# A search for row maxima moved behind both products in the attention sums of a transformer block

## The chip, the cores and the metric

The kernel runs on one core of one Trainium2 chip. The time is device microseconds of one launch, and lower is better. The five engines (TensorE or PE for matrix products, VectorE or DVE, ScalarE or ACT, GpSimd or POOL, SyncE or SP for transfers) each work through their own queue in order and wait for one another by semaphores.

## The reference, cut to what matters

The reference computes one adaptive-layernorm transformer block in float32: attention with eight heads of 32 columns over 4 batches of 2048 rows of 256, and after it a mixture of experts. The change lies in the attention:

```python
scores = jnp.einsum('bhqd,bhkd->bhqk', q, k) * scale
scores = jnp.where(causal[None, None], scores, -jnp.inf)
scores = scores + head_scales[None, :, None, None] * geo
attn = jax.nn.softmax(scores, axis=-1)
out = jnp.einsum('bhqk,bhkd->bqhd', attn, v).reshape(B, T, C)
```

Then come a second norm, two shared experts, the choice of 4 of 16 routed experts for each row, the rows' way to their experts and back, and the sum.

## The kernel before, in words

The rows are cut into 16 blocks of 512 queries, four blocks to a batch. Heads are taken four at a time (a "quad", `g` = 0 or 1). TensorE is a 128 by 128 array, and the four heads of a quad sit in four strips of it, so the four products of one kind run side by side.

Softmax is done in two passes. The **search** (`max_steps`, inner function `scores`) computes the scores of 128 queries against 512 keys with the queries in the partitions (tile `ps`), and VectorE reduces them to row maxima (tile `parts`); on the diagonal a mask is added first. One search step makes two `ps` tiles, of two heads each: eight matmul records on TensorE, then two reductions on VectorE, each behind a mask addition on the diagonal. A search covers the *next* block, so that its maxima are ready when that block's sums begin.

The **sums** (`sum_steps`) go through the keys in tiles of 128 (`kb`), with the keys in the partitions. `probabilities` (called `first` in the loop) makes the scores again into two tiles `st` of two heads each, subtracts the maxima by a further product (`mT`), and ScalarE takes the exponential of each tile into `p`. `weigh(kb, 0)` (`average`) multiplies `p` by the values into `av`, and `weigh(kb, 1)` (`total`) by ones into `dv`, which gives the softmax's denominator. Where there is room, `join` adds two `p` tiles on VectorE, and one product with ones then serves both.

All `ps` and `st` tiles, and small tiles of other steps that fall into the sums, take turns in one ring of three PSUM buffers, each of two banks (pool `mring`). So a new tile has to wait until the reader of the tile three turns earlier is done: a reduction for `ps`, an exponential for `st`.

TensorE's order is written out by hand. In the sums, each step is given a place, a number, and `run(part)` issues the steps sorted by it. A key tile owns one *slot* `n` (a whole number). Its scores stand at `n`, its product with values at `n + 1.3`, its product with ones at `n + 1.6` (or 2.55 where it is joined). So slot `m` runs: scores of tile `m`; at 0.1 a join; at 0.3 the product with values of tile `m - 1`; at 0.55 or 0.6 the product with ones; at 0.6 also the norms and the choice of experts (`put`); at 0.7 the turning of finished maxima (`turn`, tile `pr`); at 0.9 a step of the rows' transfers (`tick`).

```python
            for kb, (first, average, total) in enumerate(sums):
                n = g * half + kb
                part.append((n, first))
                part.append((n + 1.3, average))
                part.append((n + (2.55 if kb in joining else 1.6), total))
```

Between two blocks' sums stand the projections, the experts' products and most of the search (`fill_in`). Only the search steps left over there (`rest`) go into the sums; `at` spreads them over the slots. Of the 320 search steps 86 do so, in blocks 0, 1, 2, 3, 6, 7 and 10.

Of the kernel before, what the change touches and what calls it, by code (L numbers as in the profile page):

```python
# [94 lines left out]
def adaln_block_kernel(  # L95
# [1355 lines left out]
    for i in range(NBLK):  # L1451
# [4 lines left out]
        if i:  # L1456
# [21 lines left out]
            at = max(6, len(mid) - len(finals))  # L1478
# [40 lines left out]
        part = []  # L1519
        for n, (_, ss, turn) in enumerate(rest):  # L1520
            at = int(0.93 * (n + 0.5) / len(rest) * ks)
            part += [(at + 0.5, s) for s in ss]
            if turn is not None:
                part.append((min(at + 3.7, ks + 0.7), turn))
        part += [(2.7 + n, turn) for n, turn in enumerate(left)]
# [179 lines left out]
```

## Time and profile before

| | |
|---|---|
| median of 11 runs | 2458.79 us (2452.23 to 2477.46) |
| the profiled execution's own time | 2462.59 us |
| its span, first to last instruction | 2460.8 us |
| mean granted TensorE clock | 0.968 |
| TensorE busy | 2318.9 us, 94% |
| VectorE busy | 1435.1 us, 58% |
| ScalarE busy | 985.5 us, 40% |
| GpSimd busy | 732.9 us, 30% |

Every record of the main part bears line 54, since a helper class issues all instructions; so groups are told apart by tile names (`ps`, `st`, `av`, `dv`, `p`, `parts`). `PE` rows are matmuls, `PEld` rows the loading of their stationary operand. A float32 product has two matmul records for each head, so one step of four heads shows as x8. In the timeline the columns are start and duration in us, then engine, line, operation, and output<-inputs; square brackets give the idle time of the engine before the row, and what ended it.

### The profile page before, as it was taken

The numbers are of one execution on the slowest core, as the hardware profiler recorded it, in microseconds if no ns is written. First come the engines' busy times: TensorE is split into PE (matmuls) and PEld (weight loads), VectorE is DVE, ScalarE is ACT, GpSimd is POOL, SyncE is SP. The second block draws the span as 40 slices with busy tenths as digits, with TensorE's granted clock in tenths as the row PEclk, the third lists the DMA queues.
The fourth block names the chain that finished last, engine by engine and source line by source line (L and its number), as shares of the span: only waits on it lengthen the run. The fifth ranks groups of instructions, "written<-read, shape, count | busy, mean of one in ns | idle before, by whom it ended". The sixth has DMA issues, their size and how long they took to land.

```text
span 2460.8 us, 42187 instructions
## 1 busy us (share of the span) xinstructions
PE 2318.9 (94%) x16641; PEld 1134.7 (46%) x16641; DVE 1435.1 (58%) x2790; ACT 985.5 (40%) x1407; POOL 732.9 (30%) x740
## 2 busy tenths in 40 slices
PE   7999999999999999999999999997999998998998
PEld 4443433345554333354635434354544644436765
DVE  5666665536664775547665656847654675634325
ACT  2223343543334335534353344633334345552421
POOL 3201010331101344501023342601333125466325
PEclk9889999999999999999999999999999999999999
DMA  3200402243440212323524225222744844418953
GB/s 122 91 1 10 154 10 72 104 152 129 141 141 10 78 67 93 119 80 121 187 84 152 90 73 194 80 81 89 241 157 165 270 133 125 148 69 289 361 184 122
DMA packets 219830, 306.88 MB, mean 125 GB/s; under 512 B 18672, under 2 KB 158960, under 8 KB 219632
## 3 DMA queue, kind: packets, MB, share of 16 engines
q1 hardware_dynamic: 192720, 228.89, 28.1%
q0 software_dynamic: 25536, 73.43, 9.1%
q8 instruction: 131, 2.15, 0.4%
q10 hardware_dynamic: 1376, 1.86, 0.2%
q14 instruction: 67, 0.55, 0.1%
HBM read 193.49 MB, written 114.82 MB: 125 GB/s over the span
## 4 chain that ended last, share of the span: by engine, by line
PE 84%; DVE 5%; ACT 4%; issue 3%; DMA 2%; another core or an unknown queue 1%; POOL 1%; SPq 0%; ACTq 0%; DVEq 0%; POOLq 0%
PE st L54 18%; PE ps L54 13%; PE av L54 11%; PE dv L54 8%; PE pu L54 7%; PE py L54 6%; DVE parts L54 3%; PE ppq L54 3%; PE pv L54 2%; PE po L54 2%; PE px L54 2%; PE pd L54 2%; PE pd_s L54 2%; PE ppk L54 2%
## 5 line engine op out<-in xcount | busy, mean ns | idle before, releaser
L54 DVE TENSOR_REDUCE parts<-ps 128x2 f32<-128x1024 f32 (+3 forms) x640 | 662.7, 1063 | 349.0 <-PE ps L54 336.6
L54 ACT ACTIVATE p<-st 128x1024 f32<-128x1024 f32 (+3 forms) x640 | 539.1, 894 | 528.1 <-PE st L54 420.1
L54 PE MATMUL st<-qT,kv 32*128 32x512 f32 (+3 forms) x2560 | 413.9, 583 | 17.0 <-ACT p L54 12.1
L54 PE MATMUL ps<-kv,qT 32*128 32x512 f32 (+3 forms) x2560 | 381.5, 599 | 16.6 <-DVE parts L54 10.4
L54 POOL DMA_INDIRECT got<-yg,at x224 | 230.3, 1028 | 328.6 <-ACT p L54 108.2
L54 PE MATMUL av<-p,kv 128*32 128x512 f32 (+3 forms) x2560 | 305.0, 545 | 6.6 <-ACT p L54 3.2
L74 POOL DMA_INDIRECT xg<-rows,at x219 | 221.0, 1009 | 276.3 <-ACT p L54 105.5
L54 PEld LDWEIGHTS st<-qT,kv 32*128 32x128 f32 x2560 | 147.2, 186 | 276.3 <-issue 149.1
L54 PE MATMUL dv<-p,ones 128*32 128x512 f32 (+3 forms) x2224 | 255.6, 531 | 0.7 <-issue 0.7
L54 DVE TENSOR_TENSOR ps<-ps,cmask 128x256 f32<-128x256 f32 x256 | 109.3, 427 | 197.4 <-PE ps L54 162.0
L54 PEld LDWEIGHTS ps<-kv,qT 32*128 32x128 f32 x2560 | 124.3, 190 | 194.5 <-issue 87.2
L54 POOL TENSOR_TENSOR x<-x,tmps 128x512 f32<-128x512 f32 x28 | 35.4, 1263 | 493.5 <-DVE tmps L54 493.5
L54 PE MATMUL py<-wt,tact 128*128 128x256 f32 x608 | 164.3, 403 | 4.7 <-ACT xt L54 2.8
L54 PE MATMUL st<-mT,unit 3*128 3x512 bf16 (+3 forms) x1280 | 168.0, 346 | 0.0
L54 PEld LDWEIGHTS pu<-xt,wt 128*128 128x128 f32 x1216 | 149.1, 195 | 35.9 <-issue 17.8
L54 PE MATMUL pu<-xt,wt 128*128 128x128 f32 x1216 | 160.1, 284 | 2.3 <-DMA wt<-experts 1.6
L54 ACT COPY y<-py 128x512 f32<-128x512 f32 x152 | 89.0, 586 | 139.8 <-PE py L54 135.4
L54 PEld LDWEIGHTS py<-wt,tact 128*128 128x128 f32 x608 | 109.6, 195 | 55.9 <-ACT xt L54 15.5
L54 ACT COPY xt<-px 128x512 f32<-128x512 f32 x152 | 86.6, 586 | 114.3 <-PE px L54 109.3
L54 DVE TENSOR_TENSOR p<-p,p 128x1024 f32<-128x1024 f32 x84 | 105.2, 1293 | 43.2 <-PE av L54 35.7
L54 PEld LDWEIGHTS dv<-p,ones 128*32 128x32 f32 x2224 | 64.4, 110 | 133.0 <-issue 121.8
L54 POOL TENSOR_TENSOR xnb<-xnb,gm 128x256 f32<-128x256 f32 x128 | 104.8, 826 | 47.9 <-issue 19.7
(294 smaller groups left out, 2384.8 us busy)
## 6 DMA issues: line engine op xcount, KB each, us to landing
wt<-experts SPq DMA_DIRECT2D x304, 256.0 KB
xr<-xg SPq DMA_DIRECT2D x76, 512.0 KB
yg<-y SPq DMA_DIRECT2D x76, 512.0 KB
xg<-zeros SPq DMA_DIRECT2D x16, 1024.0 KB
xin<-in_x SPq DMA_DIRECT2D x16, 512.0 KB
x<-in_x SPq DMA_DIRECT2D x16, 512.0 KB
h2d<-xnb POOLq DMA_DIRECT2D x14, 512.0 KB
pre<-x POOLq DMA_DIRECT2D x14, 512.0 KB
```

The lines of the kernel that those rows point to most:

```text
L54: made = call(*args, **kwargs)
L74: made = call()
```

## The change

One number changes. A search step in the sums is placed at `at + 0.75` where it stood at `at + 0.5`:

```diff
         for n, (_, ss, turn) in enumerate(rest):
             at = int(0.93 * (n + 0.5) / len(rest) * ks)
-            part += [(at + 0.5, s) for s in ss]
+            part += [(at + 0.75, s) for s in ss]
             if turn is not None:
                 part.append((min(at + 3.7, ks + 0.7), turn))
```

In a slot it now comes behind the product with ones (0.55, 0.6), the norms and choices (0.6) and a turning (0.7), and ahead of the next tile's scores and of the transfers (0.9). In the built programs' instruction order this moves the search of 81 slots behind one product with ones (`av ps dv` becomes `av dv ps`); in four of these also behind a turning (`pr`), in three behind a small product of the choice (`pk`). The other 5 search steps of the sums stand in the first slot of a block, where no product precedes them, and keep their place. On VectorE the reductions move behind that slot's norms and choices. The orders of GpSimd's and SyncE's instructions are the same in both programs, and no instruction is added or removed.

## The prediction

> **What bounds the kernel now.** I read the page's busy shares and its chain of waits first, then the chain and the timeline inside one stretch of sums, row by row.
>
> ```profile
> PE 2318.9 (94%) x16641; PEld 1134.7 (46%) x16641; DVE 1435.1 (58%) x2790; ACT 985.5 (40%) x1407; POOL 732.9 (30%) x740
> ...
> PE 84%; DVE 5%; ACT 4%; issue 3%; DMA 2%; another core or an unknown queue 1%; POOL 1%; SPq 0%; ACTq 0%; DVEq 0%; POOLq 0%
> ```
>
> TensorE is busy 94% of the span and holds 84% of the chain that ends last. What is put into its queue, or left waiting there, is paid in full unless something else was late as well. The chain in two slots of block 6's sums that hold a search:
>
> ```profile
> 884.51 1.63 PE st L54 x10
> 886.15 0.99 PE av L54 x8
> 887.14 1.11 PE ps L54 x8
> 888.26 1.00 PE dv L54 x8
> 889.25 1.62 PE st L54 x10
> ```
>
> A slot is 4.73 us, all of it TensorE. But the scores take 1.62 us here, and 1.29 in slots without a search (chain at 1015.95), so some waiting hides in a row that counts as busy. The timeline of single rows tells which:
>
> ```profile
> 887.07 1.18 PE L54 MATMUL ps<-kv,qT 32*128 32x512 f32 x8
> 888.19 1.07 PE L54 MATMUL dv<-p,ones 128*32 128x512 f32 x8
> 888.25 1.23 DVE L54 TENSOR_REDUCE parts<-ps 128x2 f32<-128x1024 f32 x1 [1.39 <-PE ps L54]
> 889.18 1.48 PE L54 MATMUL st<-qT,kv 32*128 32x512 f32 x8
> 889.53 0.30 PEld L54 LDWEIGHTS st<-qT,kv 32*128 32x128 f32 x4
> ```
>
> The first reduction ends at 889.48 (888.25 + 1.23). Heads 0 and 1 of the next scores begin at 889.18, the loads for heads 2 and 3 at 889.53, 0.05 us after that reduction. So those two heads wait for the first `ps` tile, which held the third buffer of the ring, and they start 0.35 us after the others. From the search's start to that release are 2.46 us (889.53 - 887.07). On the diagonal it is later still:
>
> ```profile
> 1012.50 0.96 DVE L54 TENSOR_REDUCE parts<-ps 128x2 f32<-128x768 f32 x1
> ...
> 1012.90 0.30 PEld L54 LDWEIGHTS st<-qT,kv 32*128 32x128 f32 x4 [0.84 <-issue]
> ...
> 1013.58 0.22 PEld L54 LDWEIGHTS st<-qT,kv 32*128 32x128 f32 x2 [0.38 <-issue]
> ```
>
> Here the mask's addition (0.43 us, from 1012.04) stands ahead of the reduction, which ends at 1013.46; heads 2 and 3 load at 1013.58, 0.68 us behind heads 0 and 1. I went through the 81 slots in which the search will change places. In 70 the second half of the scores starts behind the first like this, by 0.17 to 2.20 us; in 4 both start together, just as that reduction ends or later; the 7 with a `pr` or `pk` between are taken singly below. The product with ones stands exactly between the search and the scores that wait for it: it is the cover.
>
> **What the change does, part by part.** It adds and removes no instruction.
>
> The cover goes. From the search's start to the release remain 2.46 us, but of TensorE's work only the search itself (1.1 us) and heads 0 and 1 are left to fill them. The next scores' second half starts about 1.4 us behind its first, for 0.35 before. The product's time comes ahead of the search and pushes search, reduction and release back by its length.
>
> How long that is, two pairs of rows tell:
>
> ```profile
> 1005.61 1.07 PE L54 MATMUL av<-p,kv 128*32 128x512 f32 x8
> ...
> 1006.49 1.90 PE L54 MATMUL dv<-p,ones 128*32 128x512 f32 x16
> ...
> 1010.01 1.06 PE L54 MATMUL av<-p,kv 128*32 128x512 f32 x8
> ...
> 1011.00 0.97 PE L54 MATMUL ps<-kv,qT 32*128 32x384 f32 x8
> ```
>
> From `av` to `dv` are 0.88 us, from `av` to `ps` 0.99: a change between the two shapes of tile costs 0.11. In the new order `av` and `dv` follow each other (0.88), then `dv` to `ps` takes 1.00, so the search starts 0.88 later, not 1.00. The second change saved, between `ps` and `st`, lies inside the wait and is worth nothing. A full slot becomes 1.27 us (scores' second half to `av`) + 0.88 + 1.00 + 2.46 = 5.61 us for 4.73. The narrower products, at 1044.9 to 1048.3, take 0.67 (384 queries), 0.45 (256) and 0.22 (128).
>
> The Trainium skill, "TensorEngine Tiling (Array Packing)", section "Key Properties", says that changing the tiling mode drains TensorE. It speaks for the change: the new order changes twice less in each slot. If both savings counted, 81 x 0.11 = 9 us would come off the sum below; the rows say that one of them falls into the wait.
>
> The sum over the 81 slots, by the width of the product: 65 x 0.88 = 57.2, 8 x 0.67 = 5.4, 5 x 0.45 = 2.3, 3 x 0.22 = 0.7, together 65.6 us. Corrections:
>
> - Four slots with a turning. Before, `pr` took a buffer behind the search, and the next scores' second half waited for the *second* reduction (3.59 us from the search's start at 327.08, 2.45 at 1384.20). After, `pr` (0.33) comes ahead: 0.88 + 0.33 + 2.46 against 3.59 is +0.1, and for the narrow one (release 1.65 after its start) +0.4. Two of each give 1.0 for the 3.5 counted: -2.5.
> - Three slots with `pk` (0.44): it was cover too, and both halves came just as the reduction ended: about +1.3, +1.3 and +0.7, for 2.6 counted: +0.7.
> - One slot (862.5) in which the search's second tile already waits for an exponential until 3.41 us into the slot: the product slips into that wait, -0.3 for +0.7: -1.0.
>
> That leaves 62.8 us. VectorE's moved steps I cost at nothing: the norms and choices at 0.6 now stand ahead of the reductions, but VectorE waited 1.39 us for the search in the row above, and that grows by 0.88; the code allots such slots 1.4 us. ScalarE is not late either: its second exponential ends 3.19 us after the scores' second half began (892.72 against 889.53), and the search that needs its first now starts 3.15 us after it, the scores that need its second 4.2 us after it. Behind the waiting scores are queued the maxima's product, `av`, `dv` and the next search, and ScalarE's exponentials, so the loss is passed on and not made up. Of waits elsewhere that a later TensorE could shorten there are few (the largest are `px` for a DMA, 4.3 us at 1478, and `pta` for ScalarE, 4.4 at 1301); I take 1.5 off.
>
> The profiled run takes 2462.6 us, so 2462.6 + 61.3 = 2523.9; it is 3.8 above the median of the runs. Against the median: **2520 us**, 2.5% slower.
>
> **The rivals.**
>
> *VectorE is late as well, or the clock falls.* If the steps now ahead of the reductions are not done when the search is, the release comes later by the rest. It decides once such work takes more than the 2.3 us (1.39 + 0.88) that VectorE would have idle. Slot 836.5 shows the size: there split, choices and a sum of rows made the reduction start 1.8 us late. Were every fifth of the 81 slots like it, 16 x 1.8 = 29 us more: 2549. Against it: no other of the 81 was late by over 0.4 us before. Likewise more stalls could lower the granted clock. It was 1.00 in the stretch from 291 to 393, where nearly every slot has the short stall, and 0.97 from 1373 to 1464. Three per cent of the 527 us of these stages is 16 us: 2536. The Trainium skill, "TensorE: Matmul & The Clock Gate", section on PSUM-queue depth-cycling, warns of micro-idles between matmul groups at bank turns; it prices none, and the 1.00 above speaks against it.
>
> *Faster.* If the second half of the scores found its buffer free in time (the reduction's end and the loads' start agreeing by chance), both changes of tile shape saved would count: 81 x 0.22 = 18 us, 2441. It decides where the stall is nil before and after. The constant 0.05 or 0.15 us from reduction to load, in slots whose reductions start anywhere from 1.2 to 3.0 us after the search, excludes chance for most.
>
> *Part is made up.* If half of the loss fell on time in which TensorE would have waited anyhow, it would be 31 us: 2490. the matmuls' named waits are short: none is over 13 us in total.
>
> *Nothing measurable* (within 0.3%, 7.4 us, about what can be told from no change here): gains and losses would have to cancel, 2459.
>
> **How the numbers follow.** My forecast: 0.77. Its lower end is 2504, 45 us (65.6, corrections doubled to -5.6, and -15 for all the waits of `px`, `pta` and `ptb` behind these blocks); its upper end 2536, 77 us (no corrections, and six slots as late as that at 836.5, 6 x 1.8). VectorE or clock, 2536 to 2560: 0.09. Part made up, 2466 to 2504: 0.08. Nothing: 0.02. Faster: 0.04. The range from 2500 to 2545 takes in the first, half of the second and the upper end of the third. Faster by over 0.3% is 0.04, within 0.02, slower 0.94.
>
> **What would show it.** In the profile after: slots such as the one at 884 should be 5.6 us long in the chain, with order `av`, `dv`, `ps`, `st`, and a score piece of about 2.7 us. The load of heads 2 and 3 should still start 0.05 us behind the first reduction's end, 2.46 us after the search began, and 1.3 to 1.4 us after heads 0 and 1. `av` to `dv` should be 0.88, the reduction's idle time ahead of it longer than 1.39. Blocks 1 and 2 and 6 and 10 should carry nearly all of the loss (13, 20, 20 and 13 slots), blocks 4, 5, 8, 9 and from 11 on none. I am wrong if the scores' second half starts with its first, if VectorE has no idle time ahead of the reductions, or if a stretch without search in its sums gets longer.

## The result, and the profile after

The changed kernel takes **2538.64 us** (median of 16 runs, 2530.56 to 2541.72). The kernel before took 2463.1 in 62 runs beside it, and the ratio is 1.0295, 95% interval 1.0274 to 1.0316: about 3% slower. The profiled execution took 2537.04 us (span 2535.3) against 2462.59 (2460.8), so there are 74.5 us of span to find.

The page of the kernel after: busy time and share by engine, the chain by engine, and the group of the scores (busy time, mean of one, then the engine's idle time ahead of it and what ended it).

```profile
PE 2338.6 (92%) x16641; PEld 1145.4 (45%) x16641; DVE 1436.4 (57%) x2790; ACT 985.1 (39%) x1407; POOL 731.5 (29%) x740
...
PE 80%; DVE 8%; ACT 4%; issue 3%; DMA 1%; another core or an unknown queue 1%; POOL 1%; SPq 0%; ACTq 0%; DVEq 0%; POOLq 0%
...
L54 PE MATMUL st<-qT,kv 32*128 32x512 f32 (+3 forms) x2560 | 451.1, 583 | 70.7 <-DVE parts L54 54.7
```

VectorE's share of the chain went from 5% to 8%, with the same busy time. The idle time ahead of the scores was 17.0 us before, most of it ended by ScalarE's `p`; now it is 70.7, and 54.7 of it ends with a reduction. The scores wait for the reduction of the search. One slot of block 6 in the chain of waits (start, length, what):

```profile
937.68 0.81 PE st L54 x4
938.49 1.00 PE av L54 x8
939.49 0.86 PE dv L54 x8
940.35 1.08 PE ps L54 x8
941.43 0.02 issue
941.45 1.24 DVE parts L54
942.69 0.04 issue
942.73 0.41 PE st L54 x2
```

The order is `av dv ps st`, as the diff says, and a reduction now stands in the chain in 73 of the 81 moved slots; before it did in 11. The next slot's `av` is at 944.08, so the slot takes 5.59 us (944.08 - 938.49) where it took 4.73. The timeline of the same slot shows who waits:

```profile
937.15 0.70 PE L54 MATMUL st<-qT,kv 32*128 32x512 f32 x2 [0.47 <-DVE parts L54]
...
938.42 1.07 PE L54 MATMUL av<-p,kv 128*32 128x512 f32 x8
...
939.30 1.04 PE L54 MATMUL dv<-p,ones 128*32 128x512 f32 x8
...
940.28 1.14 PE L54 MATMUL ps<-kv,qT 32*128 32x512 f32 x8
...
941.24 1.02 PE L54 MATMUL st<-qT,kv 32*128 32x512 f32 x4
...
941.45 1.23 DVE L54 TENSOR_REDUCE parts<-ps 128x2 f32<-128x1024 f32 x1 [1.91 <-PE ps L54]
```

From `av` to `dv` are 0.88 us, from `dv` to `ps` 0.98. Heads 0 and 1 start 0.96 after the search (941.24), heads 2 and 3 only at 942.73, which is 2.45 after the search and 1.5 after the first half. TensorE as a whole stands still for some 0.5 us of that (0.47 in the row of 937.15); for the rest half of its rows work alone. VectorE idled 1.91 us ahead of the reduction, 1.39 before: it is not late.

So far this is the predicted picture. The granted clock is not. The windows view (stretch, its length, busy time of PE, PEld, DVE, ACT, POOL, granted clock, DMA share, GB/s), for block 2's sums and for two neighbouring pieces of them:

```profile
302.00:430.00 128.00, 114.09 (x846) 38.07 (x849) 66.52 (x116) 43.92 (x52) 7.68 (x10) 0.95 0.18 61
...
400.00:403.20 3.20, 2.38 (x16) 0.61 (x16) 2.69 (x4) 0.36 (x1) 0.00 (x0) 0.99 0.00 0
403.20:406.60 3.40, 3.40 (x20) 0.81 (x16) 0.00 (x0) 1.58 (x2) 0.00 (x0) 0.51 0.00 0
```

The clock over this stretch was 1.00 before (291 to 393) and is 0.95 now. In one 3.4 us window it is about half, and that window follows 3.2 us in which TensorE was busy for only 2.38 us, 74%. The timeline of TensorE there:

```profile
401.60 0.70 PE L54 MATMUL st<-qT,kv 32*128 32x512 f32 x2 [0.82 <-DVE parts L54]
...
402.87 1.72 PE L54 MATMUL av<-p,kv 128*32 128x512 f32 x8
404.35 1.96 PE L54 MATMUL dv<-p,ones 128*32 128x512 f32 x8
406.23 1.28 PE L54 MATMUL ps<-kv,qT 32*128 32x512 f32 x8
```

A search on the diagonal, with the mask's addition ahead of the reduction, made TensorE stand for 0.82 us. After it `av` to `dv` takes 1.48 us and `dv` to `ps` 1.88, for 0.88 and 0.98.

**Where the 74.5 us are.** I measured each slot from `av` to `av` in both profiles and added up the records of the granted clock.

| part of the difference | us |
|---|---|
| the 81 moved slots, at full clock (75 slots that were at full clock in both, 55.8, scaled to 81) | +60.3 |
| 33.6 us more at half clock within the sums that hold searches (14.4 before, 48.0 after), half of it lost | +16.8 |
| other slots of the sums at full clock | -0.4 |
| the stretches between the sums | -2.8 |
| sum | +73.9 |

The second row is an upper estimate, as it takes TensorE to be the bound in all of that time. The block times (from a block's first scores to its last) bear it out: the sums of blocks 0, 1, 2, 3, 6, 7 and 10 grew by 3.0, 10.9, 21.8, 7.7, 13.9, 5.9 and 13.2 us, together 76.4, which is 16.1 more than the slots at full clock.

Not all of the second row comes from the new stalls. The clock's records change only at multiples of 3.41 us, and ten slow spells begin inside these sums. In the 3.41 us ahead of each, TensorE was busy for 43 to 76%. Seven of the ten follow a wait in a moved slot, of 0.82 to 2.28 us; they last 3.41 us each, 24 us together, 21 of them within the second row; about 10 are lost. The other three follow a wait of 1.58 to 1.81 us for ScalarE at the start of a block's sums. The kernel before has the same three waits, and in blocks 3 and 7 its clock fell behind them too. In block 2 it did not: there the wait was divided between two of the clock's windows, each 73 to 74% busy, and now it lies in one, 47% busy. An eleventh spell, at the start of block 10's sums, lasts 13.65 us for 6.83 before. A poorly filled window is not always followed by a slow one: of 34 windows in these sums with TensorE busy for 76% or less, ten were.

### The profile page after: what moved, and what is told of

It is laid out like the page before. It is cut to its first block, busy times and chain, and to the rows that moved or that the text cites. A ratio compares the mean times of both kernels' runs of the same rounds, so it can differ in the third digit from the quotient of the medians.

```text
span 2535.3 us, 42184 instructions
## 1 busy us (share of the span) xinstructions
PE 2338.6 (92%) x16641; PEld 1145.4 (45%) x16641; DVE 1436.4 (57%) x2790; ACT 985.1 (39%) x1407; POOL 731.5 (29%) x740
## 4 chain that ended last, share of the span: by engine, by line
PE 80%; DVE 8%; ACT 4%; issue 3%; DMA 1%; another core or an unknown queue 1%; POOL 1%; SPq 0%; ACTq 0%; DVEq 0%; POOLq 0%
PE st L54 17%; PE ps L54 12%; PE av L54 11%; PE dv L54 8%; PE pu L54 7%; PE py L54 6%; DVE parts L54 5%; PE ppq L54 2%; PE px L54 2%; PE pv L54 2%; PE po L54 2%; PE pd L54 2%; PE pd_s L54 2%; PE ppk L54 2%
## 5 line engine op out<-in xcount | busy, mean ns | idle before, releaser
L54 PE MATMUL st<-qT,kv 32*128 32x512 f32 (+3 forms) x2560 | 451.1, 583 | 70.7 <-DVE parts L54 54.7
L54 PE MATMUL ps<-kv,qT 32*128 32x512 f32 (+3 forms) x2560 | 374.0, 598 | 16.2 <-DVE parts L54 10.4
L54 PE MATMUL av<-p,kv 128*32 128x512 f32 (+3 forms) x2560 | 313.3, 558 | 7.4 <-issue 3.8
L54 PEld LDWEIGHTS st<-qT,kv 32*128 32x128 f32 x2560 | 156.1, 187 | 342.5 <-issue 164.0
L54 PEld LDWEIGHTS ps<-kv,qT 32*128 32x128 f32 x2560 | 118.5, 190 | 192.6 <-issue 103.3
L54 PE MATMUL st<-mT,unit 3*128 3x512 bf16 (+3 forms) x1280 | 174.5, 351 | 0.0
L54 PEld LDWEIGHTS dv<-p,ones 128*32 128x32 f32 x2224 | 74.0, 113 | 127.4 <-issue 117.2
L54 PEld LDWEIGHTS av<-p,kv 128*32 128x32 f32 x2560 | 54.2, 109 | 145.4 <-issue 119.0
```

Source lines behind the costliest of these rows:

```text
L54: made = call(*args, **kwargs)
```

## The experiments

The theories are named as in the expectations. **A**: the scores' second half waits for the first reduction, and the product with ones no longer covers that. **B**: VectorE is late, because norms and choices now stand ahead of the reductions. **C**: the new stalls make the clock fall, and that is a cost of its own. The kernel before takes from 2426 to 2469 us on the different chips of these runs, so each ratio is to the runs of the kernel before on the same chip, and times are compared only within a chip.

### VectorE's order alone, and the product's place alone

The first kernel is the one before with the norms and choices ahead of the search. On TensorE only the small products `pk` of three slots move, ahead of the search; the product with ones stays behind it.

```diff
-                part.append((at + 0.6, step))
+                part.append((at + 0.45, step))
```

> The VectorE half of the change alone: the norms and choices move from 0.6 to 0.45, ahead of the search, which stays at 0.5; on TensorE the product with ones stays behind the search. Theory A (the product with ones was cover for the wait on the first reduction): ratio to before 1.000 within 0.003; only the three small products of the choice cost about 0.4 us each. Theory B (the norms and choices ahead of the reductions make VectorE late): most of the loss, 1.02 to 1.03.

Measured: 2430.48 against 2425.59, 1.0015 (1.0002 to 1.0029). The slots at full clock sum to +0.7 us. VectorE's new order costs next to nothing; B falls.

The second is the changed kernel with the norms and choices behind the search again (`at + 0.6` to `at + 0.8`), so that against the kernel before the product with ones changes sides, and in four slots the turning, but VectorE's order does not.

> The TensorE half alone: the search at 0.75 as in the change, the norms and choices moved behind it to 0.8, so VectorE reduces ahead of them as before. Theory A: the whole loss, ratio 1.027 to 1.031 (about 2535 us). Theory B: 1.000 to 1.005.

Measured: 2500.77, 1.0314 (1.0296 to 1.0331), with +56.8 us in the moved slots at full clock, for 60.3 in the changed kernel. Nearly the whole loss comes with the place of the product. Of the other 3.5 us 1.7 stand in the three slots with `pk`, whose place differs between the two kernels.

### Shorter reductions: take the wait away

In both orders the reductions in the sums read only the first quarter of the columns, so the maxima are not those of all keys. Nothing else is touched.

```diff
-                    parts[:, t, 2 * a : 2 * a + 2, ch], both[:, :, :w], AX.X, ALU.max
+                    parts[:, t, 2 * a : 2 * a + 2, ch], both[:, :, : w // 4 if state["summing"] else w], AX.X, ALU.max
```

> The kernel before, but in the sums the reductions read only a quarter of the search's columns (the maximum is then that of a subset; the softmax's shift changes, the work on TensorE does not). The reduction falls from 1.23 to about 0.42 us, so the release comes 1.65 us after the search's start, ahead of the scores at 2.1. Theory A: the waits of 0.35 to 1.0 us of the 81 slots go, 35 to 45 us, ratio 0.981 to 0.987. Theory B: VectorE has time to spare as it is, 1.000.

> The changed kernel with the same short reductions. Theory A: the release comes 0.88 + 1.65 us after where the search used to start, 0.4 us behind the scores in plain slots and 0.9 in diagonal ones: 35 to 50 us slower than quarter_early in place of 74, ratio to before 0.997 to 1.008. Theory B (moved norms and choices): the difference stays near 74 us.

Measured against 2469.33: the early order 2434.98, 0.9853 (0.9809 to 0.9897); the late one 2460.52, 0.9965 (0.9938 to 0.9992). The two orders stand 25.5 us apart where the full reductions left some 66 to 74. A reduction of 128x256 takes 0.43 us in these runs against 1.23, which is what makes the release earlier, and with it most of the loss goes: A is shown. From the late kernel's timeline:

```profile
950.51 0.43 DVE L54 TENSOR_REDUCE parts<-ps 128x2 f32<-128x256 f32 x1
```

More of the loss went than I had expected (35 to 50 us were to be left). The slots alone differ by 36 us (+3.1 against -33.1), as expected. In the two profiled executions the late kernel spent 147 us of its span at half clock and the early one 165 (from their mean clocks, 0.970 and 0.966), which gives back about 9. Over all runs of the two the mean clocks are nearer, 0.967 and 0.965, which gives back 3 to 4; the rest of the difference between 36 and 25.5 is open.

The early kernel also shows that the order *before* was not free of this wait: 33.1 us of it were left in these slots.

### Filling the stall with useless products

If C holds, TensorE work that the answer doesn't need may make the changed kernel *faster*, as long as it lies in the stall. Here the second `ps` tile's products of each search in the sums are made twice, with the same operands into the same place:

```diff
+            if state["summing"]:
+                for u in range(2):
+                    r = G * (2 + u)
+                    nc.tensor.matmul(
+                        halves[1][:, u, :w],
+                        lhsT=qTs[i][r : r + G, g, t * P : (t + 1) * P],
+                        rhs=kT[r : r + G, (i - qb + ch) % SLOTS, g, :w],
...
+                    )
```

> The kernel before with the same doubled products. Theory A: there the wait is only 0.35 us in a plain slot and 0.6 to 1.0 in diagonal ones, so 0.6 us of the 0.96 show in some 36 plain slots and 0.2 to 0.4 in the others: 25 to 40 us, ratio 1.010 to 1.016. Without a wait 78 us, 1.032.

> The changed kernel, but in the sums the products of the search's second tile are made twice: 0.96 us more of TensorE work in each of 86 slots, between the search and the waiting scores, 0 to 83 us if all of it showed. Theory A: it falls into the 1.39-us wait, so the time is that of the changed kernel, 2538 within 6 us, ratio to before 1.028 to 1.033. If there is no wait there, 2538 + 78 = 2616, ratio 1.06. If waiting lowers the clock (theory C: the 12 us by which the forecast fell short are extra half-clock windows of 3.41 us), it could come out up to 12 us lower, with fewer such windows.

Measured: on the order before, 2450.99 against 2425.59, 1.0101 (1.0084 to 1.0118): the extra products cost 25 us. On the changed order, 2487.23, 1.0243 (1.0225 to 1.0262), which is 13.5 us *less* than the 2500.77 of the kernel with only the product moved, on the same chip. Its slots at full clock lost as much as that one's (59.0 against 56.8), so the gain isn't there; its total at half clock was 133.6 us against 162.3, and half of that difference is 14.4. The other runs agree: the mean clock over the four of each kernel is 0.975 against 0.967.

Inside the searched sums, though, the half clock had hardly moved in that pair's profiles (39.3 against 42.1); most of the difference lay elsewhere, and why isn't known. So I repeated it beside the unaltered changed kernel:

> The changed kernel, on the same chip as the next: ratio 1.028 within 0.004. Theory C: its profile again has half-clock windows that begin in the slot behind a diagonal search of 384 keys, where TensorE's records fill only 0.76 of the 3.4 us before (slots 1_1_4, 2_1_6, 3_1_5 or their like), and some 40 to 55 us of such windows in the sums that hold searches.

> The changed kernel with the search's second tile multiplied twice, as in twice_late. Theory A: the added 78 us of TensorE work cost nothing in the 81 slots, so no slower than late_third. Theory C: the windows behind the 384-key slots are gone, and the time is 5 to 14 us below late_third. If the earlier difference between two chips was the reason, the two agree within 3 us.

Measured against 2428.09: the changed kernel 2509.27, 1.0323 (1.0290 to 1.0357); with the useless products 2483.56, 1.0236 (1.0202 to 1.0269). They make it faster by 25.7 us, more than expected. The slots at full clock lose the same (57.9 and 59.0). At half clock are 180.0 us against 121.8 in all, and within the searched sums 53.3 against 6.5; half of those 46.8 us is 23.4. The windows view of the two kernels for the same stretch of the program, which holds block 2's sums, first the changed kernel, then the one with useless products:

```profile
300.00:449.00 149.00, 134.24 (x1001) 50.03 (x1003) 78.17 (x138) 49.72 (x63) 12.00 (x14) 0.95 0.17 57
```

```profile
300.00:443.00 143.00, 129.72 (x1081) 50.35 (x1079) 76.05 (x136) 49.71 (x63) 11.78 (x14) 0.99 0.16 54
```

The first has 80 matmul records fewer and takes 6 us longer, at a clock of 0.95 for 0.99. The timeline of the kernel with useless products shows where they went:

```profile
918.93 0.59 PE L54 MATMUL st<-qT,kv 32*128 32x512 f32 x2
918.95 0.59 PE L54 MATMUL ps<-kv,qT 32*128 32x512 f32 x2
...
920.43 0.70 PE L54 MATMUL st<-qT,kv 32*128 32x512 f32 x2 [0.46 <-DVE parts L54]
```

The extra `ps` products run beside the first half of the scores, in the other rows of the array, and the second half still waits for the reduction as before (0.46 us of idle time for 0.47). Stall and slot are the same in these slots, 5.59 us in the chain (on the diagonal the longest stalls fall from 1.5 or 1.7 us to 1.1); what differs is the clock. C is shown: a part of the loss is the clock's, and work in the half-empty array takes it away. Between those two kernels nothing else was changed, and it does not hang on the two profiles: the clock is 0.964 to 0.966 in the four runs without the useless products and 0.969 to 0.976 in the four with them. Not all of the 46.8 us in the searched sums is their work, though: some 20 follow waits for ScalarE at the start of a block's sums, which are as long in the other profile (1.58 to 1.81 us) and are followed by no slow window there.

### The changed kernel again

> The changed kernel again, for the comparison on one chip and for its half-clock windows: ratio 1.0295 within 0.003. Theory C (stalls bring more half-clock windows): its profile again shows some 25 us more of throttled time than the kernel before (185 to 159), several of them inside the sums of blocks 1, 2, 3, 6, 7 and 10. If that was chance, the windows in the sums go.

Measured: 2535.04 against 2469.33, 1.0253 (1.0210 to 1.0296), less than expected. The slots at full clock lost 60.1 us, as in the first profile (60.3); at half clock were 195.1 us in all and 54.8 in the searched sums. The ten slow spells of the first profile are all there again, three of them behind a search of 384 keys on the diagonal, and two more, in block 0.

But the expected 25 us of half clock more than in the kernel before did not come on this chip. The granted clock of every run is on record. Put together for all runs of a chip (half clock in us is twice the span times what the mean clock lacks of 1), it tells what the clock adds to the slots:

| kernel | mean clock, before and after | more at half clock, us | half of it | loss measured less the slots' loss |
|---|---|---|---|---|
| the changed kernel in this section (2469 us before) | 0.962, 0.963 | 3 | 2 | 65.7 - 60.1 = 5.6 |
| only the product moved (2426 us before) | 0.973, 0.967 | 37 | 18 | 75.2 - 56.8 = 18.4 |
| the changed kernel beside useless products (2428 us before) | 0.972, 0.965 | 39 | 20 | 81.2 - 57.9 = 23.3 |

The slots' loss is always taken against the one profile of the kernel before; the kernel with VectorE's order alone, at +0.7 us on another chip, shows how little the chip changes these slots. So the slots' part is the same wherever it was measured, 57 to 60 us, and the clock's part goes from nearly nothing to some 20 us. Where it adds nothing, the kernel before already spends as much time at half clock (some 186 us) as the changed one (189).

### The search ahead of both products

If the product with ones is cover, both products would cover more:

```diff
-            part += [(at + 0.5, s) for s in ss]
+            part += [(at + 0.2, s) for s in ss]
```

> The search placed the other way, at 0.2, ahead of both products. Theory A: two products (2.0 us) now cover the reduction and the next scores wait for nothing; but the search's second tile has to wait for the first exponential of the same slot, with no product to fill that: about 0.45 us a slot, 25 to 45 us slower than before, ratio 1.010 to 1.018. If cover behind the search were all that counts: faster than before by its waits, 0.983.

Measured: 2490.61 against 2469.33, 1.0088 (1.0059 to 1.0117), slower than the order before, a little less than expected. The timeline of this kernel in block 6:

```profile
905.45 1.02 PE L54 MATMUL ps<-kv,qT 32*128 32x512 f32 x4
...
906.78 1.13 PE L54 MATMUL ps<-kv,qT 32*128 32x512 f32 x4 [0.31 <-ACT p L54]
...
909.69 0.31 PEld L54 LDWEIGHTS st<-qT,kv 32*128 32x128 f32 x8 [0.84 <-issue]
```

The scores that follow now load all four heads together, so the wait of before is gone. A new one has come: the search's second tile needs the buffer that the scores left only a moment ago, and waits for ScalarE's exponential, 1.33 us behind the first tile. The slot is 5.43 us (904.26 to 909.69). Of the three places the one between the products is the fastest. In these slots the search needs a product ahead of it, for the buffer it takes, and one behind it, for the buffer it gives back.

### The mask by products: a version that beats both

The stalls left in the order before are longest on the diagonal, where VectorE adds the mask ahead of each reduction. Here TensorE adds it, by four products with a constant, for the diagonal searches of 384 and 512 keys in the sums (21 steps):

```diff
+            by_product = state["summing"] and ch == qb and w > 2 * P
...
+            if by_product:
+                for both in halves:
+                    for u in range(2):
+                        nc.tensor.matmul(
+                            both[:, u, w - P : w], lhsT=kmask, rhs=ident_b, start=False, stop=True
+                        )
...
-                if ch == qb:
+                if ch == qb and not by_product:
```

> The kernel before, but in the sums the diagonal's mask (for searches of 384 and 512 keys) is added by four small products on TensorE in place of two additions of 0.43 us on VectorE. Theory A: what counts is the time from the search's start to the end of its first reduction. It falls from 2.94 to about 2.67 us in 12 slots of 512 keys and from 2.59 to about 2.2 in 7 of 384, while TensorE's added 0.33 us lies inside the wait: 5 to 6 us faster than before, ratio 0.9975 within 0.0015. If TensorE's own work counts instead: 21 x 0.33 = 7 us slower, 1.003.

Measured: 2417.95 against 2428.09, 0.9951 (0.9934 to 0.9968). The same slot in the chain of the kernel before, then in this one:

```profile
370.26 0.99 PE av L54 x8
371.26 0.90 PE ps L54 x8
372.16 1.00 PE dv L54 x8
373.15 1.97 PE st L54 x10
```

```profile
371.23 0.99 PE av L54 x8
372.23 1.23 PE ps L54 x12
373.46 0.99 PE dv L54 x8
374.45 1.29 PE st L54 x12
```

The search costs 0.33 us more on TensorE and the scores 0.68 less: 4.51 us for 4.86. Some 19 such slots at -0.36 are 7 of the 10 us, which is already more than the 5 to 6 expected. For the rest the clock is enough: it was 0.974 over all runs against 0.972, some 11 us less at half clock. No run separates the two.

## Why the prediction was right, and where it fell short

The measured 2538.64 lies inside the range of 2500 to 2545, but 18.6 above the forecast of 2520 and 2.6 above the upper end that the sum itself gave (2536). The range holds it because it took in half of the rival with VectorE and the clock. Of the 18.6 us 4.3 are the kernel before, which took 2463.1 beside it where the forecast had set out from 2458.8.

**The cover.** Right, and shown. The release comes 2.45 us after the search's start (2.46 predicted), the second half of the scores 1.5 after the first (1.3 to 1.4), and with shorter reductions most of the loss goes.

**The price of a slot.** 5.58 to 5.59 us for the 5.61 predicted. The medians by the product's width are 0.86, 0.64, 0.43 and 0.22 us; 0.88, 0.67, 0.45 and 0.22 were put down. That only one of the two changes of tile shape would count held too: the first half starts 0.96 behind the search and not 1.06 or so, but that only makes its wait longer. Of the two readings weighed for the Trainium skill's drain of TensorE, the one by the rows was right.

**The corrections.** Turnings: +0.39, +0.06, +0.06, +0.39 (0.4, 0.1, 0.1, 0.4). Slots with `pk`: +1.33, +1.33, +0.71 (1.3, 1.3, 0.7). The slot that waited for an exponential: -0.20 (-0.3). The 81 slots together: 60.3 for 62.8.

**VectorE at nothing.** Right: its idle time ahead of the reductions grew from 1.39 to 1.91 and 2.41 us, and its new order alone measured 1.0015.

**Waits elsewhere.** The stretches between the sums became 2.8 us shorter (1.2 to 4.6, by where the sums are taken to end); 1.5 was taken off. The time at half clock outside the searched sums fell too, by 7 us (144.2 to 137.2), so how much of it the waits gave back isn't known.

**Where it falls.** Blocks 1, 2, 6 and 10 carry 59.8 of the 76.4 us, 78%: "nearly all" was too much said for 66 of 81 slots. The sums without searches stayed within some 2 us.

**The step that failed: the clock.** The sum had no term for it. In the profiled execution it was worth up to 16.8 us, some 10 of them behind the new waits; the miss there is 13.2 (74.5 measured, 61.3 predicted). It is no fixed cost: where the changed kernel was run again, it came to some 2 us. The rival that held it, "Three per cent of the 527 us of these stages is 16 us", had the size right but the wrong odds, and it was set up as another case, not as an addition to the forecast. The argument against it was "the 1.00 above speaks against it". That clock was granted to slots whose second half came 0.35 us late, with TensorE never quite idle. It said nothing of slots in which half of the array is empty for 1.5 us and all of it for 0.5 to 0.8, in some for up to 2.3. The profile before had a sign against it: behind a wait of 1.59 us for ScalarE, at 417.0 and again at 942.3, the clock fell to half for 3.4 us. The stretches that made up its 527 us begin, there, only at 423 and at 948, when most of these two spells is over. The Trainium skill, "TensorE: Matmul & The Clock Gate", section "A second HAM failure mode: psum-queue depth-cycling", was cited there and set aside. The runs side with the page: the kernel without and with TensorE work in those gaps has 53.3 and 6.5 us at half clock in the searched sums. How full TensorE must be is not settled: 76% preceded a slow window, and 54% was in one place followed by none.

**The rivals.** VectorE late: fell. Faster: fell, as the stall grew in nearly every slot. Part made up: fell, as some 200 other slots of the sums moved by 0.4 us together.

## What to carry to other kernels

A product that seems to stand in the way between a search and the next scores may be the time in which the search's buffer is read: before moving it, measure from the producer's start to the release of the buffer, and see which work is left to fill that. Where a change makes TensorE wait more often, price the clock in the sum as well, and take the evidence for it from stretches with stalls of the new length, not of the old. Where both neighbours of a step can be late, try both sides, and then shorten what the buffer's reader does.

## What the runs showed of the hardware

- The clock can fall while TensorE is mostly busy. In the changed kernel's profile a 3.4 us window at half speed followed one in which TensorE's records filled 74%, with no whole-engine pause over 0.82 us; others followed pauses of up to 2.28 us. The loss was some 1.65 us in that slot (7.2 to 7.3 us for 5.6).
- Useless matmuls in otherwise empty rows of the array cost nothing where they lay in the stall (59.0 us lost in the slots at full clock, 57.9 without), and the kernels with them were 25.7 and 13.5 us faster than those without, at 58 and 29 us less half clock.
- The same kernel took 2426 us on one chip and 2469 on another, 1.8% apart: more than several of the effects measured here. The clock is a part of that: 0.973 and 0.962, some 129 and 186 us at half clock, half of which makes 28 us, an estimate of its share in the 44.
